# When stores and loads of an attention kernel are handed to the DMA queue

## The chip, the cores and the metric

The kernel runs on one core of a Trainium2 chip. Five engines work beside one another, each through its own queue of instructions in order: TensorE (PE, matrix products), VectorE (DVE), ScalarE (ACT), GpSimd (POOL) and SyncE (SP), which here only hands transfers to the DMA engines. An instruction that has to wait for another engine or for a transfer holds everything behind it on its own engine. The metric is the device time of the whole program in microseconds, as the median of several executions.

## The reference: two attention layers on an image

The input is four images of 256 channels and 64 x 64 pixels. Layer 0 ("A" in the code) normalizes over groups of channels, makes keys and values by 2 x 2 convolutions with stride 2, so 1024 of them, and lets 4096 queries per head look at them. Layer 1 ("B") normalizes again and attends within four areas of 1024 pixels each; to its result comes a depthwise 7 x 7 convolution of the values, and a projection. Both layers add their result to their input. Cut to the core:

```python
x = x + _L0_conv_ref(_gn(x), Wq, Wk, Wv, rel_h, rel_w)
x = x + _L1_conv_ref(_gn(x), w_qkv, b_qkv, w_pe, b_pe, w_proj, b_proj)
# layer 0: softmax((q k^T + q pos^T) * scale) v, with k, v from 2x2 convolutions of stride 2
# layer 1: proj(softmax(q k^T * scale) v within an area + dwconv7(v))
```

## The kernel before

The attention of both layers is cut into units: one unit is 512 queries of 4 heads against 1024 keys, and takes 8 steps of 128 keys. There are 8 blocks (layer A of images 0 to 3, then layer B of images 0 to 3) of 16 units, so 128 units and 1024 steps. They are dealt out in 683 phases of one and a half steps. In a phase `scores` puts the products of queries and keys into PSUM (L428), ScalarE makes exponentials of them (L469 and L480), VectorE adds these up (L504) and TensorE multiplies those of the phase before with the values (L494).

Everything else is side work that a planner written in Python lays between, when the program is built: `side` holds tasks with a due time, `choose` takes the one due first among those that are `ready`, and a phase takes none, one or two parts of one. `plan` holds loads, norms and stores at fixed steps, run by `do` near the end of a phase. `phase[0]` is the number of the phase being written. So the order of instructions on each engine is fixed beforehand, and "a phase later" means later in that order; SyncE itself runs ahead until an instruction has to wait.

The side work that the change touches:

- Layer A, `store_chunk` (L675 to L679): after the residual is added to a chunk of 512 pixels, VectorE takes its statistics, and SyncE stores it to `xmid` in DRAM, from where layer B loads it.
- Layer B, `project` (L821 to L834): two products per chunk, VectorE adds bias and residual into `xm`, and after the second SyncE stores it to the output.
- `plan_values` (L948 to L1003): the values of a chunk for the depthwise convolution, per half of the channels: two memsets for the borders of `vout` (L963, L964), a product, an eviction by ScalarE (L975), then four stores, two to `vala` (L980), from where the values of the attention come, and two to `vals` (L988). `vout` has two buffers. `written` keeps the phases in which such tasks began, and `ready` of the next asks that the last but one began at least four phases ago. `stored` notes which chunks are there.
- `load_share` (L1008 to L1039): for eight channels it loads a matrix of taps, `band` (L1029), and four strips of rows, `rows` (L1032), for the convolution on TensorE. Two or three such shares may be loaded at a time; every third one of images 1 to 3 lies in the former weights (`share`). It is called three times at the end of every phase, and inside `convolve`.
- `convolve` (L1040 to L1066): 16 channels from two shares, product by product (L1048), an eviction by ScalarE into `cout` (L1059), a store to `conv` (L1060). After each of its shares is used up it calls `load_share` at once. `chained` lets the next begin six phases after its shares were asked for. `convolved` marks an image as done; `load_rest` needs it.

Tiles of a chunk (`chunk_tile`) share six buffers among all loads of 512 pixels. The loop at the end (L1159 to L1237) writes the phases.

Of the kernel before, what the change touches and what calls it, by code (L numbers as in the profile page):

```python
# [15 lines left out]
P = 128  # L16
B, C, HH, WW = 4, 256, 64, 64
N = HH * WW
CT = C // P
# [6 lines left out]
CH = 512  # L26
NCH = N // CH
RC = CH // WW
HALO = 3
# [6 lines left out]
TY, TX, NY, XT, NP, TC = 16, 2, 4, WW // 2 + 4, 88, 8  # L36
# [24 lines left out]
def direct_path(  # L61
# [18 lines left out]
    nc = tc.nc  # L80
# [226 lines left out]
    def normed(*token):  # L307

        def ready():
            return (  # L310
                token in norm_done and norm_done[token] < phase[0] and not any(of == token for of, _, _ in norms_left)
            )

        return ready

    def soon(f):

        if now[0] < 0:
            f()
        else:  # L320
            quick.append(f)

    stats, norms = {}, {}

# [226 lines left out]
    def plan_a(b, u, prep):  # L551
# [123 lines left out]
        def store_chunk(c):  # L675
            xc = xcs.pop(c)
            for t in range(CT):
                V.bn_stats(out=stats_of(("B", b))[:, t, c, :], in_=xc[:, t, :])
            nc.sync.dma_start(xmid[b][c], xc)  # L679

        for c in range(NCH):
            g = u + 2 * c
# [22 lines left out]
    def plan_b(b, u):  # L705
# [115 lines left out]
        def project(c, to):  # L821
            cv, ps = rest[c], ps_side(f"ops_{b}_{c}_{to}")
            for t in range(CT):
                product(
                    ps, lhsT=wp_sb[:, t, to * P : (to + 1) * P], rhs=cv[:, t, :], start=(t == 0), stop=(t == CT - 1)
                )
                if t == 0:
                    yield
            xm = made_x[c]
            x_to = xm[:, to, :].rearrange("p (q f) -> p q f", f=TX)  # L830
            V.scalar_tensor_tensor(x_to, by_column(ps), bproj_sb[:, to : to + 1], x_to, ALU.add, ALU.add)  # L831
            if to == 1:
                rest.pop(c)
                nc.sync.dma_start(ov[b][:, :, c * CH : (c + 1) * CH], made_x.pop(c))  # L834

        def project_last(c):

# [110 lines left out]
    def plan_values(b, c, start):  # L948

        made = {}  # L950

        def load():
            made["at"] = phase[0]
            made["h"] = chunk_tile(f"hv_{b}_{c}")
            nc.sync.dma_start(made["h"], xmid[b][c])

        def norm(t):
            normalize(("B", b), made["h"][:, t, :], made["h"][:, t, :], t)

        def values(t):  # L960
            vout = pool.tile([P, RC, TX, XT], FP, tag="vout", name=f"vout_{b}_{c}_{t}", bufs=2)
            written.append(phase[0])
            V.memset(vout[:, :, :, 0], 0.0)  # L963
            V.memset(vout[:, :, :, 1 + WW // TX :], 0.0)  # L964
            settle(("hv", b, c))
            h = made["h"]
            ps = ps_side(f"vals_ps_{b}_{c}_{t}")
            for tt in range(CT):
                product(
                    ps, lhsT=wqkv_sb[:, tt, 2, t * P : (t + 1) * P], rhs=h[:, tt, :],  # L970
                    start=(tt == 0), stop=(tt == CT - 1),
                )
                if tt == 0:
                    yield
            S.activation(  # L975
                vout[:, :, :, 1 : 1 + WW // TX], ps.rearrange("p (r x f) -> p r f x", r=RC, f=TX), AF.Identity,
                bias=bqkv_sb[:, 2, t : t + 1],
            )
            for n in range(2):
                nc.sync.dma_start(  # L980
                    vala[b][c // 2][2 * (c % 2) + n, :, 4 * t : 4 * t + 4].rearrange("c h f x -> h c (f x)"),
                    vout[:, 4 * n : 4 * n + 4].rearrange("p r f x -> p (r f x)"),
                )

            out = vout.rearrange("p r f x -> p r (f x)")
            for f in range(TX):
                at_row = (1 - f) * (XT - 1)
                nc.sync.dma_start(  # L988
                    vals[b][HALO + c * RC : HALO + (c + 1) * RC, f, t * P : (t + 1) * P, :].rearrange("r p x -> p r x"),
                    out[:, :, at_row : at_row + XT],  # L990
                )
            if t == CT - 1:
                stored[b, c] = True

        when = int(start * NKT)
        at(0, when - 5, load)
        for t in range(CT):
            at(0, when + 5 + t, lambda t=t: later(("hv", b, c), lambda: norm(t), after(("B", b), made["at"] + 6), True))
        for t in range(CT):
            task_at(  # L1000
                when + 7, 2, values, t, due=start + 4,
                ready=lambda: written[-2] + 4 <= phase[0] and normed("hv", b, c)(), lag=1 + 4 * t,
            )  # L1003

    loaded, begun_conv = {}, set()
    shares = deque((b, k) for b in range(B) for k in range(C // TC))

    def load_share():  # L1008

        if not shares:  # L1010
            return
        b, k = shares[0]
        if b not in begun_conv or len(loaded) >= (3 if b else 2):
            return
        for c in range(NCH):
            if (b, c) not in stored:
                return
        shares.popleft()
        row, size = C * XT, TC * XT
        if b and (b * (C // TC) + k) % 3 == 2:  # L1020
            place = const.tile([P, 2 * CT * 4 * C], FP, tag="wkv", name=f"share_{b}_{k}")
            n = 2 * NY * size
            xs = place[:NP, :n].rearrange("p (h y c x) -> p h y c x", h=2, y=NY, c=TC)
            band = place[:NP, n : n + 2 * TY * TX * TC].rearrange("p (h y m) -> p h y m", h=2, y=TY)
        else:
            band = pool.tile([NP, 2, TY, TX * TC], FP, tag="band", name=f"band_{b}_{k}", bufs=2)
            xs = pool.tile([NP, 2, NY, TC, XT], FP, tag="rows", name=f"rows_{b}_{k}", bufs=2)
        loaded[b, k] = band, xs, phase[0]
        nc.sync.dma_start(band, mats[k])  # L1029
        for a in range(4):  # L1030
            p = NP // 2 * (a % 2)
            nc.sync.dma_start(  # L1032
                xs[p : p + NP // 2, a // 2].rearrange("p y c x -> p y (c x)")[:, :, : size - 3],
                bass.AP(
                    tensor=vals[b].tensor, offset=vals[b].offset + k * size + a,
                    ap=[[row, NP // 2], [TY * TX * row, NY], [1, size - 3]],
                ),
            )

    def convolve(b, n):  # L1040
        size = NY * WW // TX
        ps = ps_side(f"conv_ps_{b}_{n}")
        for k in range(2):
            band, xs, _ = loaded.pop((b, 2 * n + k))
            for i in range(2):
                for half in range(2):
                    for m in range(4):
                        T.matmul(  # L1048
                            ps[HD * m : HD * m + HD, (2 * k + i) * size : (2 * k + i + 1) * size].rearrange(
                                "p (y x) -> p y x", y=NY  # L1050
                            ),
                            lhsT=band[:, half].rearrange("p y (x c) -> p (y x) c", c=TC)[:, :, 4 * i + m],
                            rhs=xs[:, half, :, 4 * i + m, : WW // TX], start=(half == 0), stop=(half == 1),
                        )
            if k == 0:
                load_share()
                yield
        out = pool.tile([P, 4, size], FP, tag="cout", name=f"cout_{b}_{n}", bufs=2)
        S.copy(out.rearrange("p i y -> p (i y)"), ps)  # L1059
        nc.sync.dma_start(  # L1060
            conv[b][16 * n : 16 * n + 16].rearrange("(i c) m y x -> (c m) i (y x)", i=4), out
        )
        load_share()
        if n == C // 16 - 1:
            convolved[b] = True
        yield  # L1066

    def plan_conv(b, n, start):
        when = int(start * NKT)
        if n == 0:  # L1070
            at(0, when - 8, lambda: begun_conv.add(b))
        def chained():
            return all(k in loaded and loaded[k][2] + 6 <= phase[0] for k in ((b, 2 * n), (b, 2 * n + 1)))

        task_at(when, 2, convolve, b, n, due=start + 2.5, ready=chained, lag=5)

# [79 lines left out]
        task(parts, g, *args, due=0.6)  # L1156
    f = step = 0
    before, credit = [], 0.0
    while f < PHASES or before or plan or side or quick or norms_left or to_add or to_divide:  # L1159
        now[0], phase[0] = step, f  # L1160
        exps = scores(f) if f < PHASES else [lambda: None] * 3
        mine = []
# [57 lines left out]
        while step < -(-3 * (f + 1) // 2):  # L1220
            do(*divmod(step, NKT))
            step += 1
        for _ in range(3):
            load_share()
        if before:
# [609 lines left out]
```

## Time and profile before

| what | us |
|---|---|
| median of 3 runs | 3063.67 (3062.66 to 3065.93) |
| the profiled execution | 3063.53 |
| its span, first to last instruction | 3061.5 |
| TensorE busy | 3032.8 |
| VectorE busy | 2526.2 |
| ScalarE busy | 2455.9 |
| GpSimd busy | 433.8 |

The span is the profiled execution without what lies around it on the device. Busy time of TensorE counts a matmul until its modelled end, so it can be near the whole span and still hide stretches in which the engine waits. In the lines of a timeline the first number is the start, the second the length, and the bracket says how long the engine had been idle and what ended that. In the lines of waits the numbers are the sum of us, how often, and the longest one. SPq is SyncE's queue; its time of issue is not counted as busy.

### The profile page before, as it was taken

The page shows a single profiled execution, that of the slowest core. Times are in us where ns is not written, and L with a number is a line of the kernel's source. Part 1 is how long each engine was busy: PE and PEld are TensorE (multiplying, and loading weights), DVE is VectorE, ACT ScalarE, POOL GpSimd, SP SyncE. Part 2 cuts the span into 40 slices and gives each one's busy share as a digit, 9 for nine tenths or more (in the row PEclk, how much of TensorE's full clock was granted, in tenths as well). Part 3 has the DMA queues.
Part 4 walks back from the last instruction along what each step waited for, and adds up shares of the span by engine and source line. Part 5 has one row for each costly group of instructions (what it writes and reads, how often), then busy time and mean ns, then how long its engine had stood idle before and what let it go on. Part 6 is the DMA issues. An engine that isn't in the chain of part 4 may idle for free.

```text
span 3061.5 us, 108320 instructions
## 1 busy us (share of the span) xinstructions
PE 3032.8 (99%) x47254; PEld 1280.0 (42%) x47254; DVE 2526.2 (83%) x2769; ACT 2455.9 (80%) x2988; POOL 433.8 (14%) x794
## 2 busy tenths in 40 slices
PE   9999999999999999999999999999999999999998
PEld 6444434444344444333444444444434444443332
DVE  3788988889887787878888888788878888888888
ACT  3888888888887888888888877788777787878885
POOL 0011111111111111111111111111111111111111
PEclk9999999999999999999999999999999999999999
DMA  5244533466354557777866677667755565553232
GB/s 191 51 101 98 126 92 73 109 142 165 83 140 133 143 152 175 189 161 194 204 175 162 156 176 185 152 171 178 176 127 145 144 159 143 149 139 79 50 71 62
DMA packets 644250, 422.73 MB, mean 138 GB/s; under 512 B 409740, under 2 KB 552572, under 8 KB 643768
## 3 DMA queue, kind: packets, MB, share of 16 engines
q1 hardware_dynamic: 619384, 380.11, 49.3%
q0 software_dynamic: 24384, 35.62, 5.1%
q8 instruction: 373, 6.11, 0.9%
q14 instruction: 109, 0.89, 0.1%
HBM read 317.28 MB, written 97.05 MB: 135 GB/s over the span
## 4 chain that ended last, share of the span: by engine, by line
PE 91%; DMA 3%; DVE 2%; ACT 2%; issue 2%; SPq 1%; POOL 0%; DVEq 0%; ACTq 0%; POOLq 0%
PE s L428 31%; PE av L494 26%; PE k0ps L167 4%; PE den L513 4%; PE v0ps L167 4%; PE q1ps L167 4%; PE k1ps L167 4%; PE conv_ps L1048 4%; PE q0ps L167 4%; PE ops L167 4%; PE vals_ps L167 3%; DVE acc L504 1%; ACT p L469 1%; DMA vals<-vout 1%; DMA rows<-vals 1%
## 5 line engine op out<-in xcount | busy, mean ns | idle before, releaser
L504 DVE TENSOR_TENSOR acc<-acc,p 128x1024 f32<-128x1024 f32 x1790 | 2117.4, 1220 | 382.7 <-PE av L494 285.7
L469 ACT ACTIVATE p<-s 128x1024 f32<-128x1024 f32 x1194 | 1159.8, 1025 | 419.3 <-PE s L428 407.6
L480 ACT ACTIVATE p<-s 128x1024 f32<-128x1024 f32 x598 | 619.8, 1036 | 1.5 <-DVE acc L504 0.7
L428 PE MATMUL s<-q,k_A 32*64 32x256 f32 (+1 forms) x10928 | 541.1, 494 | 4.1 <-ACT p L469 3.5
L428 PE MATMUL s<-q,k_B 32*64 32x512 f32 (+1 forms) x10912 | 537.1, 494 | 2.8 <-ACT p L469 2.4
L494 PE MATMUL av<-p,v_A 128*32 128x256 f32 (+1 forms) x4784 | 451.4, 486 | 0.0
L494 PE MATMUL av<-p,v_B 128*32 128x512 f32 (+1 forms) x4776 | 449.4, 487 | 0.0
L428 PEld LDWEIGHTS s<-q,k_B 32*64 32x64 f32 x10912 | 266.0, 130 | 325.1 <-PE s L428 60.4
L428 PEld LDWEIGHTS s<-q,k_A 32*64 32x64 f32 x10928 | 263.2, 130 | 329.1 <-PE s L428 58.5
L537 POOL DMA_DIRECT2D rb<-recs x508 | 251.4, 501 | 510.3 <-DMA recs<-few 497.9
L535 POOL DMA_DIRECT2D recs<-few x127 | 71.3, 561 | 1719.9 <-DVE sums L534 1600.3
L494 PEld LDWEIGHTS av<-p,v_B 128*32 128x32 f32 x4776 | 149.2, 110 | 264.5 <-issue 238.3
L494 PEld LDWEIGHTS av<-p,v_A 128*32 128x32 f32 x4784 | 149.5, 110 | 227.5 <-issue 186.0
L469 ACT ACTIVATE acc<-s 128x1024 f32<-128x1024 f32 x172 | 167.0, 1023 | 80.6 <-PE s L428 80.2
L513 PE MATMUL den<-acc,ones 128*32 128x512 f32 x1024 | 138.5, 605 | 0.9 <-DVE xm L831 0.9
L167 PE MATMUL ops<-cv,wp_sb 128*32 128x512 f32 x1024 | 126.6, 605 | 4.7 <-DVE xm L831 3.5
L527 POOL DMA_DIRECT2D few<-den_sb x127 | 90.5, 713 | 271.9 <-ACT den_sb L526 271.3
L167 PE MATMUL vals_ps<-hv,wqkv_sb 128*32 128x512 f32 x1024 | 124.9, 598 | 0.5 <-issue 0.5
L167 PE MATMUL q1ps<-h,wqkv_sb 128*32 128x512 f32 x1024 | 124.9, 599 | 0.0
L167 PE MATMUL k1ps<-h,wqkv_sb 128*32 128x512 f32 x1024 | 123.0, 597 | 1.7 <-ACT cout L1059 0.9
L167 PE MATMUL q0ps<-hq,wq_sb 128*32 128x512 f32 x1024 | 124.0, 597 | 0.1
L167 PE MATMUL k0ps<-taps,wkv 128*32 128x256 f32 x2048 | 123.9, 383 | 0.0
(102 smaller groups left out, 2089.5 us busy)
## 6 DMA issues: line engine op xcount, KB each, us to landing
rows<-vals SPq DMA_DIRECT2D x384, 195.9 KB
rb<-recs POOLq DMA_DIRECT2D x508, 64.0 KB, 3.6
share<-vals SPq DMA_DIRECT2D x128, 195.9 KB
vala<-vout SPq DMA_DIRECT2D x128, 144.0 KB
vals<-vout SPq DMA_DIRECT2D x128, 144.0 KB
vc<-vala SPq DMA_DIRECT2D x64, 288.0 KB
band<-mats SPq DMA_DIRECT2D x96, 176.0 KB
hq<-in_x SPq DMA_DIRECT2D x32, 512.0 KB
```

The costliest lines, as they stand in the source:

```text
L167: T.matmul(out[cols, :], lhsT=lhsT[:, cols], rhs=rhs, start=start, stop=stop)
L428: T.matmul(out[n : n + WIDE], lhsT=unit[2]()[rows, unit[0], j * P + n : j * P + n + WIDE], rhs=unit[1]()[rows, cols], start=True, stop=True,)
L469: S.activation(p, (a, b)[n], AF.Exp, scale=SCALE)
L480: S.activation(p, c.rearrange("p b (l n) -> p b l n", l=2), AF.Exp, scale=SCALE)
L494: T.matmul(out, lhsT=v[:, j, unit[0] * P + HD * h : unit[0] * P + HD * h + HD], rhs=rhs, start=(j == 0 and not u), stop=(j == NKT - 1), sk ...
L504: V.tensor_add(to, to, p)
L513: T.matmul(dens[g][HD * h : HD * h + HD, :], lhsT=ones, rhs=p(h), start=(n == 0), stop=(n == len(sets) - 1),)
L527: G.dma_start(few[:, 0, :], den_sb[0:P:HD, :].rearrange("h (q n) -> h q n", n=CH // HD))
L535: G.dma_start(recs.rearrange("h (q n) -> (h q) n", n=CH // HD), few[:, 1, :])
L537: G.dma_start(rb[HD * h : HD * h + HD, :], recs[h : h + 1, :].to_broadcast([HD, CH]))
L1048: T.matmul(ps[HD * m : HD * m + HD, (2 * k + i) * size : (2 * k + i + 1) * size].rearrange("p (y x) -> p y x", y=NY), lhsT=band[:, half].r ...
```

## The change

A small list `posts` is added. `post(n, f)` puts an action off for `n` phases, and `hand_out` does those that are due, at the end of each phase, after the plan's loads of that phase and before the three calls of `load_share`. Before the phases begin, `post` acts at once. The loop goes on until nothing is left in `posts`.

With it, the store of `xmid` and that of the output are written two phases later, the four stores of `vout` and the store of `cout` one phase later; `stored` and `convolved` are set with the stores. `load_share` is no longer called inside `convolve`; a share whose products were written in this phase still counts as loaded (`freed`), so the load that takes its place is written at the end of the next phase at the earliest. Three constants go along: values begin five phases after the last but one, in place of four, and `chained` asks for five phases after the load, in place of six. The two stores of the very last chunk (L860) stay where they are.

```diff
+    def post(n, f):
+        if now[0] < 0:
+            f()
+        else:
+            posts.append((phase[0] + n, f))
+
+    def hand_out():
+        due = [f for at, f in posts if at <= phase[0]]
+        posts[:] = [(at, f) for at, f in posts if at > phase[0]]
+        for f in due:
+            f()
...
-            nc.sync.dma_start(xmid[b][c], xc)
+            post(2, lambda: nc.sync.dma_start(xmid[b][c], xc))
...
-                nc.sync.dma_start(ov[b][:, :, c * CH : (c + 1) * CH], made_x.pop(c))
+                made_x.pop(c)
+                post(2, lambda: nc.sync.dma_start(ov[b][:, :, c * CH : (c + 1) * CH], xm))
...
+            def store():
                 (the four stores of vout, and stored[b, c] = True after the second half)
+            post(1, store)
...
-                ready=lambda: written[-2] + 4 <= phase[0] and normed("hv", b, c)(), lag=1 + 4 * t,
+                ready=lambda: written[-2] + 5 <= phase[0] and normed("hv", b, c)(), lag=1 + 4 * t,
...
-        if b not in begun_conv or len(loaded) >= (3 if b else 2):
+        if b not in begun_conv or len(loaded) + sum(f == phase[0] for f in freed) >= (3 if b else 2):
...
+            freed.append(phase[0])
             if k == 0:
-                load_share()
                 yield
...
-        nc.sync.dma_start(conv[b][...], out)
-        load_share()
-        if n == C // 16 - 1:
-            convolved[b] = True
+        post(1, store)      # the store of cout, and convolved[b] after the last
...
-            return all(k in loaded and loaded[k][2] + 6 <= phase[0] for k in ((b, 2 * n), (b, 2 * n + 1)))
+            return all(k in loaded and loaded[k][2] + 5 <= phase[0] for k in ((b, 2 * n), (b, 2 * n + 1)))
...
+        hand_out()
         for _ in range(3):
             load_share()
```

More of the change, by code (lines that the diff above doesn't have):

```diff
@@ L321, in soon @@
             quick.append(f)
+    posts = []
+    def post(n, f):
[8 more added lines that the diff above has]
+            f()
     stats, norms = {}, {}
@@ L978, in values @@
             )
[L979 to L993, printed above, removed]
+            def store():
+                for n in range(2):
+                    nc.sync.dma_start(
+                        vala[b][c // 2][2 * (c % 2) + n, :, 4 * t : 4 * t + 4].rearrange("c h f x -> h c (f x)"),
+                        vout[:, 4 * n : 4 * n + 4].rearrange("p r f x -> p (r f x)"),
+                    )
+                out = vout.rearrange("p r f x -> p r (f x)")
+                for f in range(TX):
+                    at_row = (1 - f) * (XT - 1)
+                    nc.sync.dma_start(
+                        vals[b][HALO + c * RC : HALO + (c + 1) * RC, f, t * P : (t + 1) * P, :].rearrange("r p x -> p r x"),
+                        out[:, :, at_row : at_row + XT],
+                    )
+                if t == CT - 1:
+                    stored[b, c] = True
+            post(1, store)
         when = int(start * NKT)
@@ L1001, in plan_values @@
                 when + 7, 2, values, t, due=start + 4,
-                ready=lambda: written[-2] + 4 <= phase[0] and normed("hv", b, c)(), lag=1 + 4 * t,
+                ready=lambda: written[-2] + 5 <= phase[0] and normed("hv", b, c)(), lag=1 + 4 * t,
             )
-    loaded, begun_conv = {}, set()
+    loaded, begun_conv, freed = {}, set(), []
     shares = deque((b, k) for b in range(B) for k in range(C // TC))
@@ L1059, in convolve, with store @@
         S.copy(out.rearrange("p i y -> p (i y)"), ps)
-        nc.sync.dma_start(
-            conv[b][16 * n : 16 * n + 16].rearrange("(i c) m y x -> (c m) i (y x)", i=4), out
-        )
-        load_share()
-        if n == C // 16 - 1:
-            convolved[b] = True
+        def store():
+            nc.sync.dma_start(
+                conv[b][16 * n : 16 * n + 16].rearrange("(i c) m y x -> (c m) i (y x)", i=4), out
+            )
+            if n == C // 16 - 1:
+                convolved[b] = True
+        post(1, store)
         yield
@@ L1158, in direct_path @@
     before, credit = [], 0.0
-    while f < PHASES or before or plan or side or quick or norms_left or to_add or to_divide:
+    while f < PHASES or before or plan or side or quick or norms_left or posts or to_add or to_divide:
         now[0], phase[0] = step, f
```

## The prediction

> **What bounds the kernel now.** I read the page's first part, then the waits of each engine, then SyncE's own waits, then the timeline where waits for DMA appear. First the page: busy time of each engine, and that in 40 slices.
>
> ```profile
> span 3061.5 us, 108320 instructions
> ...
> PE 3032.8 (99%) x47254; PEld 1280.0 (42%) x47254; DVE 2526.2 (83%) x2769; ACT 2455.9 (80%) x2988; POOL 433.8 (14%) x794
> ...
> DMA  5244533466354557777866677667755565553232
> ```
>
> TensorE has something under way 99% of the time; VectorE and ScalarE are at 83% and 80%. The 1024 key-tile steps of attention are dealt out, one and a half to a phase, in 683 phases, so 3061.5 / 683 = 4.5 us each, and a phase is TensorE's sequence: scores, up to two parts of side work, weighted sums. SyncE's own waits, the longest first, are of another size:
>
> ```profile
> SPq L1029 <- PE conv_ps L1048: 308.4, 41, 19.3
> SPq L834 <- DVE xm L831: 264.1, 18, 40.2
> SPq L679 <- DVE xc L673: 207.3, 15, 27.3
> SPq L980 <- DVE vout L964: 109.0, 20, 17.6
> ```
>
> These are the four places that the change moves: 308.4 + 264.1 + 207.3 + 109.0 = 888.8 us, 29% of the span, in which SyncE stands before one instruction with the rest of its queue behind it. The question is how much of that anybody feels. The waits of the compute engines for a DMA answer it: over the whole run VectorE waits 6.5 us for `vals<-vout`, ScalarE 3.9 us for the same and 2.0 us for `hq<-in_x`. So I looked at the phases themselves. The phase length is the distance of two starts of scores (L428). TensorE's timeline just before the worst place shows the normal ones:
>
> ```profile
> 1302.41 1.55 PE L428 MATMUL s<-q,k_A 32*64 32x256 f32 x32
> ...
> 1306.18 1.54 PE L428 MATMUL s<-q,k_A 32*64 32x256 f32 x32
> ...
> 1310.80 1.54 PE L428 MATMUL s<-q,k_A 32*64 32x256 f32 x32
> ...
> 1354.32 1.54 PE L428 MATMUL s<-q,k_A 32*64 32x256 f32 x32
> ...
> 1359.00 1.55 PE L428 MATMUL s<-q,k_A 32*64 32x256 f32 x32
> ```
>
> One side part: 1306.18 - 1302.41 = 3.77 us. Two parts: 4.62. A convolution: 4.68. Against these the timeline of 1380 to 1403 us has
>
> ```profile
> 1380.92 1.55 PE L428 MATMUL s<-q,k_A 32*64 32x256 f32 x32
> ...
> 1383.23 0.81 ACT L392 ACTIVATE hq<-hq,norm_A 128x512 f32<-128x512 f32 x1 [2.04 <-DMA hq<-in_x]
> ...
> 1385.92 2.00 PE L428 MATMUL s<-q,k_A 32*64 32x256 f32 x32 [1.17 <-ACT p L469]
> ...
> 1388.28 0.70 ACT L975 ACTIVATE vout<-vals_ps,bqkv_sb 128x512 f32<-128x512 f32 x1 [1.50 <-DMA vals<-vout]
> 1388.33 0.07 DVE L963 MEMSET vout<- 128x16 f32 x1 [4.70 <-DMA vals<-vout]
> ...
> 1392.24 1.98 PE L428 MATMUL s<-q,k_A 32*64 32x256 f32 x32
> ...
> 1397.47 1.55 PE L428 MATMUL s<-q,k_A 32*64 32x256 f32 x32
> ```
>
> A late `hq` and a late store of `vout` hold ScalarE, it holds the exponentials and the eviction, and TensorE stops. Going through all phases, those that are longer than their content explains by over half a microsecond, and touch a DMA[...], are seven. Excess of each (start to start, less 3.77, 4.62 or 4.68):
>
> - 1240.81 to 1246.86, convolution: 6.05 - 4.68 = 1.37 (`vout` waited 2.4 us for its old store)
> - 1359.00 to 1365.14, two parts: 6.14 - 4.62 = 1.52 (weight load without a releaser, 1.39 us of "issue")
> - 1380.92 to 1385.92, one part: 5.00 - 3.77 = 1.23 (`hq`)
> - 1385.92 to 1392.24, convolution: 6.32 - 4.68 = 1.64 (`vout`)
> - 1392.24 to 1397.47, two parts: 5.23 - 4.62 = 0.61 (the next `hq` behind the late ScalarE)
> - 1397.47 to 1402.03, one part: 4.56 - 3.77 = 0.79 (VectorE behind after its 4.70)
> - 1501.08 to 1506.38, convolution: 5.30 - 4.68 = 0.62 ("issue" again)
>
> Sum 7.78 us: 5.64 from late DMA with its echo, 2.14 from "issue". That is all the change can take back by its own logic, out of 888.8.
>
> **What the Trainium skill says.** Perfetto Trace Analysis, Identifying the Most-Contended Engine, warns that matmul busy time is no measure of headroom since matmuls are pipelined; this trace agrees, PE shows 99% busy with phases of 3.77 and 6.32 us in it, which is why I count by phases. DMA: Bandwidth & Descriptors, Anatomy of one DMA, says that DMA engines don't wait for semaphores, the issuing sequencer does before it dispatches; the four waits above are exactly that. Its section Queues, rings and completion order has descriptors consumed in ring order on each engine, so a store handed over behind loads is also moved behind them; here `vals<-vout` issued at 1378.61 landed 9.48 us later by the chain of waits, behind `rows<-vals` issued at 1369.19 (9.40 us). Perfetto Trace Analysis, Per-instruction lifecycle, puts the wait outside the profiled window of an issue: the 5.20 us of the two L988 at 1377.46 are then hand-over into a busy DMA, not waiting for data.
>
> **The change, part by part.** No compute instruction is added or removed: same matmuls, activations, adds. The DMAs are the same in number and size too: 32 `xmid<-xc`, 31 `out<-xm`, 128 `vala<-vout` and 128 `vals<-vout`, 64 `conv<-cout`; 96 `band`, 32 `share<-mats`, 384 `rows`, 128 `share<-vals`. Only their place in SyncE's queue moves.
>
> *xmid and out stores, two phases later.* Their data are ready about one phase after the old place, so SyncE stops for them less and loads queued behind go out sooner, up to two phases (9 us). No engine waited for those loads except at 1381; worth 0 elsewhere, covered by the 4 to 6 phases the planner already leaves between a load and its first use (over 17 us). The price: chunk buffers are held longer. One end: nothing, other end: a load into the buffer waits one phase more; I take nothing, the planner's slack covers it.
>
> *vout store, one phase later, and the next use of its buffer one phase later (written + 5).* Near 1230 and 1376 SyncE reached the store late anyhow: it was still handing over shares (1369.19 to 1373.7, 4.49 us for four `rows`). In the new order conv store and shares also precede it, so the store goes out at about the same time while the memset that waits for it comes 4.6 us later. Waits of 2.4, 1.5 and 4.70 us are all at or about covered by that: 1.37 + 1.64 + 0.79 gone. The tighter rule touches only tasks that began exactly four phases after the last but one; from the `vals_ps` in the timeline those are 7 of 64. They swap with other side work, so no part is added: 0.
>
> *conv store one phase later, shares taken at the phase's end, one phase after the convolution.* The longest stop (308.4 us) goes. Readiness is counted as load + 5 instead of + 6, with the load one phase later, so the next convolution may still start six phases after the last. The `hq` load at 1374.67 stood behind two shares; taken a phase later, these come after it, and `hq` lands several us earlier: 1.23 + 0.61 gone. What lies nearer to the edge now are the shares: at 1369.19 they had 9.40 us to landing and were used at 1389.03, so 10.4 us to spare, of which a phase (4.6) is taken.
>
> *The end.* The last but one `out<-xm` (issued 3044.41) is now handed over after the final two halves (3053.48), before the last one (3055.74). DMA moved 262 GB/s while that store ran (3045 to 3047), so its 512 KB are 2.0 us of data; they fill the gap of some 1 us and push the last store by about 1 us: +1.0, between 0 and 2.
>
> *"Issue".* The changed order of the bursts may help or not: between 0 and -2.14, more if it hurts; I take half, -1.07.
>
> Sum: -(1.37 + 1.64 + 0.79) - (1.23 + 0.61) - 1.07 + 1.0 = -5.7 us, against the profiled execution's own 3063.53 (span 3061.5 and 2.0 around it): 3057.8. The median of the runs is 0.14 above it, so 3057.9; of the waits that follow a phase with no side work (2956.42 to 2961.50, two parts, 5.08 - 4.62 = 0.46 us) one should fall to the swaps: 3057.5.
>
> **Rivals.** (1) *Bursts keep their lateness.* Between 1200 and 1600 us the DMA share is 0.67 to 0.82 and single hand-overs take 3 us; if the stores now stand behind still more loads, they land a phase later as well, and what was won by + 5 is lost. For it: ring order. Against: loads pull ahead by less than what SyncE lost in waits. Then only `hq` improves and the end pays: 3063.5 - 1.2 + 1.0, some 3063.5. (2) *More is won.* All seven excesses go (-7.8) and with VectorE and ScalarE no longer late some five of the 0.46 us waits too: about 3053.5. For it: 888.8 us of stops is a lot of disturbance; against: outside 1240 to 1510 the trace shows no wait for DMA that reaches TensorE. (3) *Slower: shares arrive late.* TensorE takes convolutions in order; if the two shares are not there five phases after hand-over (21 us), each late one stops scores directly. Its place is batch 1, 1360 to 1660 us, 16 convolutions at a DMA share of 0.72 to 0.82. It decides once landing takes 10.4 - 4.6 = 5.8 us more than now; at 0.6 us each that is 16 x 0.6 = 10 us, 3073. For it: landings of 8 to 9.5 us in the chain. Against: nothing in the trace of before waits for `rows`, `band` or `share`, so the true slack is unseen but positive. (4) That the change does nothing is included in (1): the queue order does change.
>
> **Chances.** Forecast 0.62, own range 3055 to 3060.5; no change (1) 0.11; more (2) 0.12; slower (3) 0.15. Faster by over 0.2% means under 3057.5 (6.1 us; about what a measurement of this kernel can tell from no change): half of the forecast's case and a little more, 0.33, with (2) 0.45. Slower by over 0.2% is (3) and a little of (1): 0.16. The rest, 0.39, is within. The range 3053 to 3066 leaves out most of (3) and the far end of (2), less than 2 in 10.
>
> **What would show it.** Right: SyncE's waits for `conv_ps`, `xm`, `xc` and `vout` shrink from 888.8 us to a few hundred at most; ScalarE's and VectorE's waits for `vals<-vout` and `hq<-in_x` (12.4 us together) vanish; phases around 1240 and 1380 to 1400 are 4.7 us or less; TensorE's group times stay as they are. Wrong: new waits of `conv_ps` for `rows` or `band`, or of `hq`, `taps` and `st_A` for chunk loads; waits for `vals<-vout` still there; a longer stretch after 3053 us than the 8 us of now.

## The result and the profile after

| | before | after |
|---|---|---|
| median | 3062.66 us (3059.31 to 3065.93, 5 runs) | 3082.53 us (3075.84 to 3083.43, 5 runs) |
| ratio | | 1.0057, 95% interval 1.0046 to 1.0069 |
| span of the profiled execution | 3061.5 us | 3081.5 us |

The change makes the kernel slower by 0.57%, some 17 us; the profiled executions are 20.0 us apart. Below, "before" and "after" are the two kernels, and every ratio is against the kernel before, run on the same chip at the same time. Line numbers are those of the changed kernel unless "before" stands beside them.

The page of after, the same three lines as in the prediction:

```profile
span 3081.5 us, 108330 instructions
...
PE 3039.7 (99%) x47254; PEld 1278.9 (42%) x47254; DVE 2526.6 (82%) x2769; ACT 2456.1 (80%) x2988; POOL 435.3 (14%) x794
...
DMA  5243543366345557777877676766755565653222
```

VectorE and ScalarE do the same work in the same time, and no slice of DMA differs by more than one. TensorE's busy time is 6.9 us longer for the same 47254 matmuls; why is shown below. The rest of the 20 us is standing. SyncE's own waits of after (sum, times, longest, in us):

```profile
SPq L1082 <- ACT cout L1079: 313.7, 40, 18.3
...
SPq L850 <- DVE xm L846: 255.1, 15, 38.2
...
SPq L694 <- DVE xc L688: 157.8, 13, 20.4
...
SPq L998 <- DVE vout L980: 76.8, 14, 17.6
...
SPq L971 <- PE vals_ps L167: 17.0, 2, 8.8
...
SPq L971 <- PE q0ps L167: 15.6, 3, 10.2
```

The four stops that the change aims at were 888.8 us and are 313.7 + 255.1 + 157.8 + 76.8 = 803.4. The largest, 308.4 us before a share could be loaded, has not gone: the conv store now stands ahead of the share and waits for the same convolution. The last two lines have grown: a load of `hv` (L971) waits for its chunk buffer 32.6 us in all, before it was 6.2 + 2.9. And the waits of the compute engines for a DMA, after:

```profile
DVE vout L979 <- DMA vals<-vout: 9.3, 3, 6.0
DVE st_A L579 <- DMA xs<-in_x: 8.3, 3, 7.2
...
PE conv_ps L1068 <- DMA rows<-vals: 5.2, 4, 2.5
...
ACT vout L991 <- DMA vals<-vout: 3.0, 1, 3.0
PEld conv_ps L1068 <- DMA rows<-vals: 3.0, 2, 1.5
```

`rows` is new: in before no product of the convolution waited for it. `vout` has 12.3 us where before had 10.4, at other places, and `xs` 8.3 us where before had 3.9. Where two engines wait for one transfer, such sums count it twice.

**Where the 20.0 us are.** The phases of both traces, taken as in the prediction (start to start of scores, against phases of like content), give four terms. The first phase starts 0.7 us earlier. The excess of all phases over their content (the time that a phase takes beyond a normal one with the same work in it) goes from 29.3 to 44.0 us: +14.7. The phases are dealt out a little differently (five more without a side part, six fewer with one, one more with two and one more with four): +4.3. From the start of the last phase to the end of the span it is 29.8 us in place of 28.1: +1.7. Together 20.0.

The +14.7 is a difference of gains and losses. The excesses from 1359 to 1402, 5.8 us of the prediction's list, are gone. In their place stand mainly these:

- 611.3: 1.8 us, a write into `vout` waits for its old store
- 705.0: 3.4 us, VectorE waits for `xs`; 713.0: 3.1 us, in which TensorE waits for nothing but is slow (see the clock, below)
- 1247.2: 12.8 us, of which 8.1 us excess (before 1.4), the convolution waits for `rows`, 5.0 us in all, and is slow afterwards
- 1435.9 and 1517.0: 1.7 and 2.3 us, `vout` again, and a weight load that nothing in the trace releases

The largest one, timeline of after, 1229 to 1260 us (start, length, instruction; in brackets the idle time before and what ended it):

```profile
1229.68 1.78 SPq L108 DMA_DIRECT2D hq<-in_x  x1
...
1239.77 0.34 SPq L971 DMA_DIRECT2D hv<-xmid  x1
...
1240.20 0.39 SPq L1082 DMA_DIRECT2D conv<-cout  x1
1240.64 0.90 SPq L1049 DMA_DIRECT2D band<-mats  x1
...
1241.59 1.77 SPq L1052 DMA_DIRECT2D rows<-vals  x4
...
1244.38 3.32 SPq L1052 DMA_DIRECT2D rows<-vals  x4
...
1247.18 2.00 PE L443 MATMUL s<-q,k_A 32*64 32x256 f32 x32 [0.37 <-ACT p L484]
...
1250.74 0.89 PE L1068 MATMUL conv_ps<-rows,band 88*32 88x128 f32 x24 [1.18 <-DMA rows<-vals]
...
1254.15 0.46 PE L1068 MATMUL conv_ps<-rows,band 88*32 88x128 f32 x8 [2.51 <-DMA rows<-vals]
...
1255.95 1.52 PE L1068 MATMUL conv_ps<-rows,band 88*32 88x128 f32 x24 [1.34 <-DMA rows<-vals]
...
1257.21 2.81 PE L509 MATMUL av<-p,v_A 128*32 128x256 f32 x16
```

The same two shares and their convolution in before:

```profile
1217.87 0.37 SPq L1029 DMA_DIRECT2D band<-mats  x1
...
1224.86 3.27 SPq L1032 DMA_DIRECT2D rows<-vals  x4
...
1243.65 1.99 PE L1048 MATMUL conv_ps<-rows,band 88*32 88x128 f32 x64 [1.30 <-ACT vout L975]
```

After `hq` SyncE hands over nothing for 8.3 us: it stands before the `hv` load, whose chunk buffer is still read by the product of the values (L167). The store of the convolution and both shares stand behind it and go out from 1240.20 to 1247.70. The convolution that uses them begins at 1249.11 and waits strip by strip. In before they were handed over from 1217.87 to 1228.13 and used at 1243.65: 15.5 us from the end of the hand-over to the first product, against 1.4 now. The Trainium skill (DMA: Bandwidth & Descriptors, Anatomy of one DMA) says that a DMA's wait is served by the issuing sequencer before dispatch; this is that sentence with a price, since a load that waits for a buffer holds back loads that wait for nothing.

A second thing paces SyncE, in both kernels. Its transfers use eight completion semaphores in turn, so each of them waits until the one eight places ahead of it has landed. In before SyncE waits so some 530 times, some 340 us in all. A merged line such as `rows` x4 with 3.32 us is therefore four hand-overs of 0.28 us with such waits between them. The strips of the second share wait one after the other for the landings of `hv`, of the conv store, of `band` and of the first strip, all of which went out behind the late `hv`.

The second place, timeline of after, 690 to 716 us:

```profile
690.52 1.24 SPq L998 DMA_DIRECT2D vala<-vout  x2
...
691.80 3.22 SPq L1006 DMA_DIRECT2D vals<-vout  x2
...
695.07 2.91 SPq L953 DMA_DIRECT2D mats<-made  x1
...
698.02 3.81 SPq L944 DMA_DIRECT2D made<-bands  x3
...
701.94 0.47 SPq L971 DMA_DIRECT2D hv<-xmid  x1
...
704.20 0.47 SPq L108 DMA_DIRECT2D xs<-in_x  x1
...
708.90 0.69 DVE L579 BATCH_NORM_STATS2 st_A<-xs 128x6 f32<-128x512 f32 x1 [7.16 <-DMA xs<-in_x]
...
710.81 2.16 ACT L484 ACTIVATE p<-s 128x1024 f32<-128x1024 f32 x2 [3.53 <-DVE acc L519]
...
713.02 3.31 PE L443 MATMUL s<-q,k_A 32*64 32x256 f32 x32 [3.34 <-ACT p L484]
```

The same place in before:

```profile
681.53 1.15 SPq L980 DMA_DIRECT2D vala<-vout  x2
...
695.43 0.33 SPq L955 DMA_DIRECT2D hv<-xmid  x1
...
697.56 0.47 SPq L108 DMA_DIRECT2D xs<-in_x  x1
```

Four late transfers of `vout` take 4.5 us of hand-over in front of `hv` and `xs`, and the `mats` store right behind them takes 2.91 us where it took 0.92. In before the last store of `vout` ahead of them was at 681.53, and `hv` went out at 695.43, `xs` at 697.56; now 701.94 and 704.20. VectorE waits 7.16 us for `xs`, the exponentials for VectorE, the scores for the exponentials.

**The clock after a stop.** The trace also holds the clock that TensorE was granted, as a share of full speed. In after it is 0.50 in two stretches of 6.83 us, from 712.1 and from 1254.8 us, at these two stops; in before it is full throughout from 75 to 3040 us. The lines show it: the scores at 713.02 take 3.31 us and the weighted sums at 1257.21 2.81 us, where 1.55 and 1.47 are normal. Half of the time that TensorE worked in the two stretches, 5.9 and 5.7 us, is 2.9 us each (an estimate), so some 6 of the 14.7 us are not the stops but what follows them. That fits its busy time, 6.9 us longer. a_only, w5, share_first and b_w6 (below) have no such stretch between 75 and 3000 us; each of the other kernels has one to five, every one at a stop.

### The profile page after: what moved, and what is told of

Its sections match the earlier page's. It is cut to its first block, busy times and chain, and to the rows that moved or that the text cites. A ratio compares the mean times of both kernels' runs of the same rounds, so it can differ in the third digit from the quotient of the medians.

```text
span 3081.5 us, 108330 instructions
## 1 busy us (share of the span) xinstructions
PE 3039.7 (99%) x47254; PEld 1278.9 (42%) x47254; DVE 2526.6 (82%) x2769; ACT 2456.1 (80%) x2988; POOL 435.3 (14%) x794
## 4 chain that ended last, share of the span: by engine, by line
PE 90%; DMA 3%; DVE 2%; issue 2%; ACT 2%; SPq 1%; POOL 0%; ACTq 0%; DVEq 0%; POOLq 0%
PE s L443 31%; PE av L509 26%; PE k0ps L167 4%; PE conv_ps L1068 4%; PE den L528 4%; PE q1ps L167 4%; PE v0ps L167 4%; PE k1ps L167 4%; PE q0ps L167 4%; PE ops L167 3%; PE vals_ps L167 3%; DVE acc L519 2%; ACT p L484 1%; DMA rows<-vals 1%; DMA vals<-vout 0%
## 5 line engine op out<-in xcount | busy, mean ns | idle before, releaser
L167 PE MATMUL ops<-cv,wp_sb 128*32 128x512 f32 x1024 | 126.6, 605 | 5.3 <-DVE xm L846 4.1
L167 PE MATMUL k0ps<-taps,wkv 128*32 128x256 f32 x2048 | 124.8, 386 | 1.7 <-ACT vout L991 1.7
L167 PE MATMUL vals_ps<-hv,wqkv_sb 128*32 128x512 f32 x1024 | 124.2, 598 | 1.3 <-issue 1.3
L167 PE MATMUL k1ps<-h,wqkv_sb 128*32 128x512 f32 x1024 | 123.0, 597 | 1.9 <-ACT k_B L748 1.2
L167 PE MATMUL q1ps<-h,wqkv_sb 128*32 128x512 f32 x1024 | 124.9, 599 | 0.0
L167 PE MATMUL q0ps<-hq,wq_sb 128*32 128x512 f32 x1024 | 124.0, 597 | 0.0
```

Of the source, the lines that this page charges most:

```text
L167: T.matmul(out[cols, :], lhsT=lhsT[:, cols], rhs=rhs, start=start, stop=stop)
```

## The experiments

**The change taken apart.** Three kernels with one part each, and the new rule for the values alone.

```diff
 a_only: before, and
+            post(2, lambda: nc.sync.dma_start(xmid[b][c], xc))
+                post(2, lambda: nc.sync.dma_start(ov[b][...], xm))
 b_only: before, and
+            post(1, store)                          # the four stores of vout
+                ready=lambda: written[-2] + 5 <= phase[0] ...
 c_only: before, and
+        post(1, store)                              # the store of cout
+            freed.append(phase[0])                  # shares at the phase's end, one phase later
+            return all(k in loaded and loaded[k][2] + 5 <= phase[0] ...
 w5: before, and
+                ready=lambda: written[-2] + 5 <= phase[0] ...
```

> Only the stores of xmid and of the output two phases later; everything else as before. Queue theory (the loss is made of a few transfers that now stand behind others in SyncE's queue: shares behind hv at 1247, hv and xs behind vout stores at 702, vout stores behind loads at 611 and 1436): these two stores are at none of the places, so -2 to +3 us. Buffer theory (chunk buffers held two phases longer make later loads wait, SyncE with them): +8 to +15 us, and more of SyncE's waits before L108 and the hv load. Order theory (side work dealt out differently): 0, since no ready rule changes.

> Only the four stores of vout one phase later and the rule of five phases. Queue theory: +6 to +10 us, the stops near 611, 702 to 720 and 1436 are there, the one of 8 us at 1247 is not. Buffer theory: about 0. Order theory: +5 to +10, and the same in the kernel with the rule alone.

> Only the store of cout and the loads of shares one phase later. Queue theory: +6 to +10 us, nearly all in one convolution around 1245 that waits for rows; SyncE's 300 us before the shares appear before the store of cout instead. Buffer theory: about 0. Order theory: about 0 to +2, the convolutions may begin at the same distances.

> Stores and loads as before, only the rule that values begin five phases after the last but one in place of four. Queue theory: -4 to 0 us, since the old store has a phase more to land: the waits for vals<-vout (10.4 us of ScalarE and VectorE together before) shrink. Order theory: +5 to +10 us, with more phases that have no side work (43 before, 48 after the change).

Measured: a_only 3062.27 us, 1.0011 (1.0004 to 1.0017). b_only 3081.69, 1.0073 (1.0060 to 1.0087). c_only 3067.11, 1.0028 (1.0019 to 1.0038). w5 3060.55, 1.0005 (0.9996 to 1.0013).

In us that is +3, +22, +9 and about +2, the last not told apart from nothing. For b_only every reading had expected at most +10, and the places that cost most were not among those named. Two theories fall here. Dealing the work out in another order costs nothing to speak of: w5 has the mix of phases of after (the same 4.3 us more) and 2.1 us of waits of `vout` where before had 10.4, its excess falls from 29.3 to 24.2 us, and the two cancel. Holding the chunk buffers longer costs little: in a_only the end of the span is 1.1 us longer, and its trace has no new stall of over 1 us. The late stores of `vout` alone cost as much as the whole change. The timeline of b_only shows how:

```profile
1385.71 1.81 SPq L998 DMA_DIRECT2D vala<-vout  x2
...
1387.57 5.15 SPq L1006 DMA_DIRECT2D vals<-vout  x2
...
1390.77 1.54 PE L443 MATMUL s<-q,k_A 32*64 32x256 f32 x32
...
1397.98 0.70 ACT L991 ACTIVATE vout<-vals_ps,bqkv_sb 128x512 f32<-128x512 f32 x1 [7.79 <-DMA vals<-vout]
...
1398.04 0.07 DVE L979 MEMSET vout<- 128x16 f32 x1 [6.46 <-DMA vals<-vout]
...
1404.51 1.54 PE L443 MATMUL s<-q,k_A 32*64 32x256 f32 x32
```

It is the place of the prediction's worst phase. In before the two stores to `vals` of this buffer were handed over from 1377.46 and the phase began at 1385.92; here it is 1387.57 and 1390.77. The store is 10.1 us later, the phase that needs the buffer 4.9. ScalarE waits 7.79 us in place of 1.50, and the phase takes 1404.51 - 1390.77 = 13.74 us, 9.1 over its content: TensorE stands for 7.1 us of it, and from 1399 to 1403 us its clock is 0.50. Another pair like it, at 1447 and 1457, has 8.6 us, and the place at 704 to 719 us has 5.8 (6.5 in after).

**Pairs of parts.**

```diff
 ac: after, and
-            post(1, store)                          # the stores of vout
+            store()
-                ready=lambda: written[-2] + 5 <= phase[0] ...
+                ready=lambda: written[-2] + 4 <= phase[0] ...
 bc: after, and
-            post(2, lambda: nc.sync.dma_start(xmid[b][c], xc))
+            nc.sync.dma_start(xmid[b][c], xc)       # and the out store likewise
```

> The change without its late vout stores (store at once, rule back to written+4); the xmid, out and conv stores and the shares stay late. Before is about 3060. If the late vout store carries the loss and the late shares only their own part: 3065 to 3071, with the stall of the convolution near 1240 (6 to 8 us) still there, no wait of vout for vals<-vout over 4 us in sum, and no stall at 705 to 720. If the parts only hurt together, in a full queue: 3059 to 3063. If every late store costs about the same: 3073 to 3077.

> The change without its late xmid and out stores (vout stores, conv stores and shares late). Alone, the late vout stores cost 22 us and the late shares with the conv store 8 us, all together 19 to 22 us. If one backlog of SyncE is paid for by whichever tile is short first: 3078 to 3084, with waits both for rows and for vals<-vout. If the two add up: 3088 to 3092. If the xmid stores in front of the shares are needed for the full loss: 3066 to 3074.

Measured: ac 3079.75 us, 1.0057 (1.0041 to 1.0074). bc 3079.99, 1.0055 (1.0039 to 1.0072).

Without its late `vout` stores the change costs the same, and without its late `xmid` stores too. For ac the 17 us are at the upper end of its last reading (13 to 17 us over a before of 3060); for bc the first came true, with waits for `rows` and for `vals<-vout` both there. The parts don't add up: 3 and 9 alone give 17 together, 22 and 9 alone give 17 together. For ac its trace shows one place where that happens. SyncE's timeline, ac:

```profile
1198.21 2.92 SPq L694 DMA_DIRECT2D xmid<-xc  x1
1201.18 0.43 SPq L1082 DMA_DIRECT2D conv<-cout  x1
1201.71 0.87 SPq L1049 DMA_DIRECT2D band<-mats  x1
1202.63 2.09 SPq L1052 DMA_DIRECT2D rows<-vals  x4
1206.21 0.29 SPq L1049 DMA_DIRECT2D band<-mats  x1
1206.92 3.06 SPq L1052 DMA_DIRECT2D rows<-vals  x4
```

Both late stores have come to stand in front of the late shares. The convolution begins at 1214.62 and waits 0.49 and 2.59 us for `rows`, the next one, at 1245.77, 3.9 us. In c_only, whose `xmid` store went out at 1187.74, only the conv store stands in front: the last strip is handed over by 1206.75 in place of 1209.98, and the convolution, at 1214.11, does not wait. So a part that costs little alone pushes one that is on the edge. The 2.92 us are not the `xmid` store's own, though: in c_only the conv store takes 2.99 us at the same place (more on this at the end).

**The shares.** When they are asked for, alone and within ac.

```diff
 c_share: c_only, and
-        post(1, store)                              # the store of cout
+        store()
 share_first: c_share, and in the loop over the phases
+        for _ in range(3):
+            load_share()
         while step < -(-3 * (f + 1) // 2):
             do(*divmod(step, NKT))
             step += 1
         hand_out()
-        for _ in range(3):
-            load_share()
 ac_early: ac, and
-            freed.append(phase[0])
+                load_share()                        # inside convolve and after its store, as before
-            return all(k in loaded and loaded[k][2] + 5 <= phase[0] ...
+            return all(k in loaded and loaded[k][2] + 6 <= phase[0] ...
```

> Only the late shares (asked for after the phase in which a buffer came free, chained+5); the conv store is handed over at once, all else as before. If the late shares carry the 6 us stall of the convolution near 1240: 3065 to 3069, waits of conv_ps for rows of 4 us or more in sum. If it was the conv store, which stands ahead of the shares in the late form: 3058 to 3062, and no wait of conv_ps for rows.

> Only the late shares, but asked for ahead of the plan's own loads of the phase in which they fall due, so that no hv load that waits for its chunk buffer stands in front of them on SyncE. If the place behind hv is what makes a share late: handed over before 1229 and not at 1227.6 to 1235.5, the stall near 1240 falls from 5.8 us to under 2 us, 3060 to 3064. If one phase later is too late by itself: 3065 to 3069 and the stall stays above 4 us.

> The change without its late vout stores, and with the shares asked for as before (chained+6): only the xmid, out and conv stores are late. With the late shares the same kernel was at 3079.75 against 3062.93 of before. In its trace the xmid store of 2.92 us and the conv store stand right in front of a share at 1198 to 1201.6, and the convolution at 1214 waits for that share. If the late shares are what this kernel pays for: 3061 to 3066, no wait of conv_ps for rows over 1 us in sum. If the backlog is only passed on to the next tile: 3074 to 3081, with waits of vout for vals<-vout of over 10 us.

Measured: c_share 3067.87 us, 1.0015 (1.0006 to 1.0024). share_first 3067.75, 1.0007 (0.9999 to 1.0016). ac_early 3069.19, 1.0015 (1.0007 to 1.0022).

The stall near 1240 is the shares' own: c_share has it with 5.8 us (conv_ps waits 5.0 us for `rows`). Handed over ahead of the plan's loads, they go out from 1224.38 in place of 1227.62, and the stall is 2.8 us: about half of it is the place behind `hv`, the rest is that a phase later is late. The whole times of the two kernels are not clearly apart. Of share_first's two expectations neither came true whole: its time lies in the second range, its stall in neither. How much of c_only's 9 us is the conv store (c_share has 5 without it) the intervals leave open. In ac_early no convolution waits for `rows`; of 17 us some 5 are left. These look passed on: the convolution's phase at 1382 has 3.9 us of excess and begins with a write into `vout` that waits 4.2 us, which ac, stopped twice before, doesn't have.

**The two buffers of vout.**

```diff
 b_w6: b_only, and
-                ready=lambda: written[-2] + 5 <= phase[0] ...
+                ready=lambda: written[-2] + 6 <= phase[0] ...
 after_w6: after, and the same
 after_early: after, with the shares as in ac_early
 early_w6: after_early, with written[-2] + 6
```

> Only the late vout stores, with written+6 in place of written+5. Of the 22 us that this part costs alone, the stalls at 1391 (9.1 us) and 1447 to 1464 (8.6 us) begin with a write into vout that waits for vals<-vout. Buffer theory: they go, 3063 to 3067, and the stalls at 704 to 719 (5.8 us, waits for xs) stay. Queue theory: the late transfers stand before the next chunk's loads whatever the rule: 3078 to 3083, the stalls come back as waits for xs, hv or hq at the same places.

> The changed kernel with the rule for the values' tasks at written+6 in place of written+5: the two vout buffers get back one phase between the handing over of a store and the next write. Buffer theory: the 15 us of waits of vout for vals<-vout fall to under 4 us and 3 to 6 us of time come back: 3076 to 3079; the stalls at 705 to 720 (6.5 us) and 1247 (8.1 us) stay, since they are waits for xs, hv and rows. Queue theory alone: 3081 to 3084, the waits of vout stay. If the later tasks cost phases of their own: over 3085.

> The changed kernel with the shares asked for as before (chained+6), written+5 kept, all stores late. Its stalls by cause were about 9 us for rows and 10 us for vout, xs and hv. Two-cause theory: the 9 us come back and no more, 3070 to 3076, with waits of vout for vals<-vout. If the two causes can stand in for each other (the late vout stores alone cost 22 us): 3078 to 3084, the stall moves to vout near 1390 or 1450. If the shares are all of it: 3060 to 3066.

> The changed kernel with the shares asked for inside the convolution as before (chained+6) and with written+6; all four kinds of store stay late. Two-cause theory (late shares reach the convolution too late, and the two vout buffers are a phase short): both causes are gone, 3060 to 3068, no wait of conv_ps for rows over 1 us. Queue theory (late stores in front of the loads cost by themselves): 3073 to 3083, waits for xs, hv or hq of 8 us or more in sum.

Measured: b_w6 3067.28 us, 1.0016 (1.0009 to 1.0023). after_w6 3081.36, 1.0061 (1.0044 to 1.0078). after_early 3088.97, 1.0076 (1.0060 to 1.0093). early_w6 3073.41, 1.0029 (1.0019 to 1.0039).

One phase more between a store and the next write of its buffer takes 17 of the 22 us away from the late `vout` stores; the stalls at 1391 and 1447 are gone, one of 2.4 us at 1458 is there, and the waits for `xs` stop TensorE from 680 to 697 us (4.7 us, in b_only 5.8 from 704 on). In the whole change the same edit brings nothing: the waits for `vals<-vout` fall from 12.3 to 4.1 us, but the `hv` load then stands until 1243.26, the shares go out after it, and the convolution's excess at 1244 is 13.9 us in place of 8.1. The opposite edit, early shares, brings nothing either, against all three expectations: no wait for `rows` is left, and `vout` waits 37 us. The timeline of after_early, at the place of b_only above:

```profile
1395.09 1.54 PE L443 MATMUL s<-q,k_A 32*64 32x256 f32 x32
...
1403.52 0.70 ACT L991 ACTIVATE vout<-vals_ps,bqkv_sb 128x512 f32<-128x512 f32 x1 [9.01 <-DMA vals<-vout]
1403.57 0.07 DVE L979 MEMSET vout<- 128x16 f32 x1 [7.68 <-DMA vals<-vout]
...
1410.75 1.54 PE L443 MATMUL s<-q,k_A 32*64 32x256 f32 x32
```

The phase takes 15.66 us (8.3 of them TensorE stands, then its clock is 0.50); in after, whose convolution had stopped 150 us earlier for `rows`, no phase between 1370 and 1410 waits for `vout`. So the two stand in for each other: whichever tile runs short first stops TensorE, and after that stop the next one is in time. That the stop lets SyncE catch up is the reading that fits; the runs show only the exchange. Both edits together bring half of the loss back. What is left in early_w6 (some 9 us) shows as waits of `vout` (15.4 us, at 1303 and 1462), of `xs` (8.6 us, around 680 to 718) and `hq` (5.1 us); whether a further phase would take them away was not tried.

**The place within a phase.**

```diff
 after_first: after, and in the loop over the phases
+        hand_out()
+        for _ in range(3):
+            load_share()
         while step < -(-3 * (f + 1) // 2):
             do(*divmod(step, NKT))
             step += 1
-        hand_out()
-        for _ in range(3):
-            load_share()
```

> The changed kernel with what is due (late stores, then shares) handed over ahead of the plan's own loads of the same phase, and not after them. If a late transfer suffers from its place behind hv, hq and xs: the waits for rows (8.2 us) fall to under 4 us, 3070 to 3078. If the plan's loads then pay for it, being behind the stores: waits for hv, hq and xs of over 15 us in sum, 3080 to 3090. If place within a phase is nothing: 3081 to 3084.

Measured: 3074.14 us, 1.0032 (1.0022 to 1.0042). As late in phases as after, but ahead of the plan's loads of `hv`, `hq` and `xs`: 0.8 us of waits for `rows` are left of 8.2, the phase at 1250 has 0.8 us of excess, and `xs` and `taps` pay a part of it (9.9 and 4.1 us). Of the whole loss about 8 us is the place behind the plan's loads of the same phase.

**A third buffer.** The room for it was taken from `vc`, the values' tile of layer B.

```diff
 before_v3: before, and
-            vout = pool.tile([P, RC, TX, XT], FP, tag="vout", ..., bufs=2)
+            vout = pool.tile([P, RC, TX, XT], FP, tag="vout", ..., bufs=3)
-            vcs[a, n] = pool.tile([P, 2, 4 * TX, XT], FP, tag="vc", ..., bufs=4)
+            vcs[a, n] = pool.tile([P, 2, 4 * TX, XT], FP, tag="vc", ..., bufs=3)
 b_v3: b_only, and the same
```

> The kernel before with three vout buffers, the room taken from the tile vc (three buffers in place of four); order of work and rules as before. Its waits of vout for vals<-vout, 10.4 us, go. Buffer theory: the stalls at 1240, 1386 and 1397 that begin with them are 3.8 us, so 3.5 to 5 us faster, ratio 0.9984 to 0.9990, unlike the rule written+5, which took the same waits away but cost about 4 us of other phase lengths. If SyncE's backlog is passed on to hq, hv or xs: ratio 0.999 to 1.001. If make_v then waits for vc: above 1.001.

> Only the late vout stores with written+5, with three vout buffers (vc three in place of four). With two buffers this is 1.0073 of before, with stalls at 611, 1391 and 1447 to 1464 that begin at a write into vout (19 us), and at 704 to 719 at xs (5.8 us). Buffer theory: the first go, 1.001 to 1.003, and the waits of vout for vals<-vout are under 2 us. Backlog theory: as slow as with two, 1.005 to 1.008, waits of hv, hq or xs of over 15 us take their place.

Measured: before_v3 3079.29 us, 1.0058 (1.0044 to 1.0072). b_v3 3096.02, 1.0103 (1.0087 to 1.0118). All waits for `vals<-vout` are gone in both, and both are slower. The first line of SyncE's waits of before_v3 says why:

```profile
SPq L742 <- DVE v_B L749: 256.3, 15, 34.6
```

With one `vc` less the load of the next one (L742) waits for VectorE's transposes, up to 34.6 us at a time, a line that the kernel before doesn't have; the new stalls lie at 1467, 1997 and 2217 us, behind it. As a test of the buffer this is confounded. What can be read: against before_v3 the late stores cost 1.0103 / 1.0058 = 1.0045 where they cost 1.0073 with two buffers, and the stalls at 611, 1391 and 1447 are gone, while that at 702 to 719 stays (8.2 us). How much of the 22 us is the buffer alone stays open between that (some 9 us) and the 17 us of b_w6. None of the kernels tried is faster than before; w5 and share_first are not told apart from it.

## Why the prediction was wrong

The forecast was 3057.5 with a range to 3066; it is 3082.53. The step that failed is that stores of `vout` and shares written a phase later would still be in time: it stood in the sum with -3.8 us and with no loss, and the parts alone measured +22 us (b_only) and +9 us (c_only). Point by point:

- **The list of seven excesses** was right as a list. Of 7.8 us those from 1359 to 1402, 5.8 us, went away in after, and so they did in w5 with the rule written + 5 alone: none of them is left there but 0.8 us at 1391. That the 1.5 us of "issue" at 1359 went with them may be luck, since nothing shows its cause.
- **"They swap with other side work, so no part is added: 0"** was wrong. The rule costs 4.3 us of phase lengths, in w5 and in after alike, and so cancels what it brings: in w5 the excess fell by 5.1 us. The term was mis-sized by more than the 3.8 us that it was meant to win.
- **"The store goes out at about the same time"** is how it failed for `vout`. From the end of `vout`'s eviction to the first hand-over of its store the kernel before has 5.6 us on average in the first 1200 us and 5.4 from 1200 to 1520; after has 8.9 and 8.3. What counts are single places: b_only has 4.9 on average from 1200 to 1520, yet for the phase at 1391 the store was 10.1 us later and the phase itself only 4.9. And the hand-over of `hv` and `xs` behind it, which the step didn't count, moved by 6.5 us at 695. b_only prices the step: +22 us where -3.8 stood.
- **"10.4 us to spare, of which a phase (4.6) is taken"** failed twice. The 10.4 was read at one place. At 1240 before had 15.5 us from hand-over to use, and c_share shows strips still landing 9.7 us after the end of theirs, so about 6 were to spare (an estimate from these two). And a phase in the program's order is not 4.6 us on SyncE's queue: against before the shares' hand-over ended 7.4 us later in c_share, while their convolution came 3.4 us earlier, and 19.6 us later in after, its convolution 5.5 us later.
- **"The longest stop (308.4 us) goes"**: it moved to the conv store, 313.7 us. The store waits for the convolution as the share had, and the share is behind it.
- **"Hand-over into a busy DMA, not waiting for data"** misread two merged lines. Of the 5.20 us at 1377.46, 0.66 are a wait for the landing of the `rows` from 1369.19, eight places ahead; of the 4.49 us for four `rows` at 1369.19 some 3.2 are such waits. So the 9.40 and 9.48 us that follow each other in the chain of waits are this pacing and say nothing of ring order; the section of the Trainium skill cited for it (DMA: Bandwidth & Descriptors, Queues, rings and completion order) also says that a later transfer may finish its write before an earlier one. The two excesses put to "issue" stay unexplained: no trace shows what released these weight loads.
- **xmid and out stores: 0** was near (a_only +3 us, the end +1.1 of it, forecast +1.0). What it left out is that a late store also stands in front of something: together with the late shares it costs 9 us and not 3 (ac against c_only), though with the `vout` stores late as well nothing more (after against bc).
- **The third rival**, shares that come late, had the right sign and the right tile. Its place was wrong (1240 in image 0's convolutions, not 1360 to 1660), and its form: one stop of 8.1 us and not sixteen of 0.6. It alone could not have given the time: it is 9 us in c_only, the `vout` waits were counted as won, and the lowered clock behind a stop was in no term.

The common error: a wait on SyncE was taken for slack that a reorder sets free. Of the 888.8 us of stops only 18.4 lie between 1200 and 1520 us in before (15.9 before a `vout` store, 2.5 before a share), and that is where all seven excesses lie. There SyncE had next to nothing to win: its hand-overs take 237 of the 320 us, and waits for the landing of the transfer eight places ahead some 50 more. The sum of the stops hardly moved (888.8 to 803.4), and transfers that nobody had waited for were pushed to where somebody does.

## What to carry to other kernels

Before a hand-over is moved later in a queue, take for each tile the time from the end of its hand-over to its first use at the tightest place, and count not the phases by which it is moved but the instructions that then stand ahead of it, above all one that waits for a buffer. Waiting time on the queue's own engine, summed over the run, is no reserve: look at the stretch where the stalls are. Where hand-overs and waits for earlier landings fill 287 of 320 us, as here from 1200 to 1520 us, what is put off is late. Price a stop of several us on TensorE with the slow stretch behind it, here some 3 us each. And test the parts in pairs: the loss of one can be hidden behind the stall of another, so that undoing either brings nothing.

## What the runs showed that was not expected

A stall can pay for others: after_early, with the convolution's 8 us stall removed, is no faster than after (1.0076 against 1.0057, the intervals overlap), and has 37 us of waits for `vals<-vout` in place of 12. The same transfers took very different times to hand over: a 512 KB store of a chunk took 0.35 us at 1440.46 in b_only and 2.92 at 1198.21 in ac. What differs is what stands in front of it: in ac the two stores to `vals`. In before the transfer handed over right behind such a pair takes 2.8 us (the median of 64); `hv`, `xmid` and `band` each take about as long there, and 0.37, 0.35 and 0.39 us elsewhere (medians after 560 us). At one place it was `xmid` with 2.92 us in ac, the conv store with 2.99 in c_only and `band` with 2.90 in c_share. So a pair of `vals` stores costs the queue its own hand-over and some 2.4 us of the next transfer's, and it is this that late `vout` stores lay in front of a load.
